# Another order for the first block of layer 1, between a full attention and a full expert network

## The chip, the cores and the metric

The kernel runs on one core of one Trainium2 chip. The metric is the time of the whole program on the device, in microseconds, as the median of three runs. The engines of the core are named as in the profile: PE is TensorE's matrix multiplication (PEld its loading of weights), DVE is VectorE, ACT is ScalarE, POOL is GpSimd, SP is the engine that issues most transfers. Each engine works off its own instructions in the order of the program and waits for the others by semaphores.

## The reference, cut to what matters

The input x has 32 rows of 128 tokens with 256 features, 4096 tokens in all. Layer 0 is attention with 8 heads over all tokens. Its output is projected (`out_w`) and added to x. Layer 1 works on the result t, in two steps, each behind a normalisation over the features:

```python
# layer 0, end
ctx = jnp.einsum('bhqk,bkhd->bqhd', attn, V).reshape(Bz, L, Dz)
dec = (ctx @ out_w.T + out_b).reshape(Bz, Nz, Tz, Dz)
x = h + alpha * dec
# layer 1, attention in a window of 24 tokens
t = x.reshape(1, 4096, 256)
key = jnp.einsum('btd,de->bte', ln(t), K)
logits = relu(jnp.einsum('btd,bsd->bts', key, ln(t)) + bias[0])
logits = (logits - 10000.0 * (1.0 - window)) * temperature[0]
t = t + jnp.einsum('bts,bsd->btd', softmax(logits), ln(t))
# layer 1, eight experts of three layers each, weighted by a softmax per token
z = ln(t)
w = softmax(z @ Wr + br)
h = relu(bn1(einsum('bfd,edh->bfeh', z, W1) + b1))
h = relu(bn2(einsum('bfeh,ehk->bfek', h, W2) + b2))
y = einsum('bfeh,ehd->bfed', h, Wo) + bo
t = t + jnp.einsum('bfed,fe->bfd', y, w)
```

`bn` is a scale and a shift per expert and feature, `g * (h - m) / sqrt(v + 0.001) + b`. All arithmetic is in 32-bit floating point.

## The kernel before, in words

**Stages.** The tokens lie in 32 tiles of 128 and in 8 blocks of four tiles (`TPB` is 4). Layer 0's attention is a list of steps (block of queries, group of four heads, tile of keys): `scores` (L1250) multiplies, `exps` (L1265) takes exponentials on ACT, `add` sums them on DVE, and `product` (L1295) multiplies with the values two steps later. In the last block some keys are masked, and POOL sets their exponentials to zero (L1275) before the product. After the last product, `evacuate` copies the attended heads to `big_t`, `close_sums` (L1322) adds up the exponentials on PE, and for this last unit the division is done in three parts, `invert_last` and `scale_last`, for tiles 0 to 4, 5 to 11 and 12 to 31.

Behind that stands the first block of layer 1, written out by hand (L2104 to L2200). It takes twelve tiles through the projection of layer 0 and tiles 0 to 3 through the whole of layer 1's attention to the first layer of the first expert. From then on a loop over 64 pieces of work (a block and an expert) runs. It issues the expert products, and between them, by a planner that reckons with fixed costs and due times, the jobs that prepare the next blocks. The planner knows nothing of measured times, so its order is the same whenever the loop begins.

**The steps of the hand-written block.** `project_half(n, c, ...)` (L1594) multiplies tile n's feature half c with the projection; two halves add up in PSUM. `second(n)` does the half c = 1, which needs the last unit's division. `complete(n)` (L2114, by `finish`, L1608) adds the result to the tokens on DVE and takes their mean and variance. `deviations(ts, 0)` is epsilon and the square root (DVE, ACT), `deviations(ts, 1)` the reciprocal and `nmr`, the negative mean times it, which `normalise` (L1624) on ACT uses. `normalise` also sends the 16 rows at each edge of a tile to its neighbours' buffers by two transfers (SP for the first five tiles, POOL later). `turn` transposes on PE and copies on ACT, `key` multiplies with K, `scores1` and `logits` (L1661, L1672) give the windowed scores of a tile and their maximum on DVE, `exponentials` (L1693) runs on ACT. `turn_weights(p)` (L1699) transposes the weights of two tiles and copies them to `pt`, two parts on ACT and a small third on DVE. `apply` (L1714) multiplies them with the tokens, and `attended` adds the result to the tokens and takes mean and variance again. `expert_tokens` (L1760, tile `xf`) normalises on DVE, `turn_tokens` (L1773) transposes to `xfT`, `layer_halves` (L1844) multiplies two tiles at a time with the first expert's first weights and ends in two rectifiers (`relu`, L1881), `route` (L1787) computes the softmax's inputs and copies them to `lgT` on DVE. `batch_norms` (L1746) makes scale and shift of the batch norms: one square root on ACT, a reciprocal on DVE and four operations on POOL. Behind these in POOL's order stand `with_bias` for tiles 12 to 15 and the weight sums of the first two experts (L1540), whose results SP stores (`kept`). `warm` issues transposes whose results nobody reads.

**PSUM.** Its eight banks are held by four tiles: `one_a` (bank 0), two tiles of three banks, and `one_b` (bank 7). The tiles of three banks are, in turn, the last scores, the sums, `three_a` and `three_b`; a tile takes the place of one whose readers are done. The framework that writes the semaphores keeps the order of two engines' accesses to a PSUM tile. `open_banks` (L1497) closes these pools and opens two others of four banks each; a first write to a new pool waits for the readers of the old ones.

**ACT's tables.** Exponential and square root need different tables. A load stands in front of the first activation that needs another table than the last; copies, rectifiers and scalings run with either.

Of the kernel before, what the change touches and what calls it, by code (L numbers as in the profile page):

```python
# [823 lines left out]
def fast_kernel(ctx: ExitStack, tc: tile.TileContext, ins: dict, out: bass.AP, narrow):  # L824
# [92 lines left out]
    last_parts = []  # L917
    with ExitStack() as l0:
# [296 lines left out]
        with ExitStack() as at:  # L1215
# [167 lines left out]

            stat_at = {
# [17 lines left out]
            for n in range(len(steps) + LAG + 1 + 16):  # L1402
# [22 lines left out]
                if 0 <= n - LAG < len(steps):  # L1425
                    product(*steps[n - LAG])
# [61 lines left out]


    one_a = ps_a.tile([P, BLK], F32, tag="a", name="one_a")  # L1490
    one_b = ps_av.tile([P, BLK], F32, tag="av", name="one_b")
    three_a, three_b = (
        ps_b.tile([P, HG - 1, BLK], F32, tag="b", name=f"three{k}") for k in range(2)
    )
# [78 lines left out]
    def deviations(ts, part):  # L1573
# [8 lines left out]
        nc.vector.reciprocal(rstd0[:, cols], rstd0[:, cols])  # L1582
        nc.vector.scalar_tensor_tensor(
# [9 lines left out]

    def project_half(n, c, ps, start):  # L1594
        nc.tensor.matmul(
            ps, lhsT=big_t[:, c, SIDE + n * P : SIDE + (n + 1) * P], rhs=woT[:, c, :],
            start=start, stop=(c == 1), skip_group_check=True,
        )
# [100 lines left out]
    def turn_weights(p, ps=None):  # L1699
# [11 lines left out]
        nc.vector.tensor_copy(pt[: 4 * SIDE, 2, :], ps[: 4 * SIDE, 2 * P : 3 * P])  # L1711
# [33 lines left out]

    def batch_norms():  # L1746
        def bnp(s):
            k = bn_names.index(s) * 2 * E
            return bnT[:, :, k : k + 2 * E]

        rstd_of(bscale, bnp("v"), 1e-3)
        nc.gpsimd.tensor_tensor(bscale, bscale, bnp("g"), op=ALU.mult)
        nc.gpsimd.tensor_tensor(bshift, bnp("b"), bnp("m"), op=ALU.subtract)
        nc.gpsimd.tensor_tensor(bshift, bshift, bscale, op=ALU.mult)
        nc.gpsimd.tensor_tensor(bshift, bshift, bnp("be"), op=ALU.add)
# [31 lines left out]
    def route(b):  # L1787

        xfT = blk[b]["xfT"]
        ps = bank(f"psr{b}")[:, :P]  # L1790
# [305 lines left out]
    def half(ps, k):  # L2096
        return ps[:, k * D : (k + 1) * D]

    def first_halves(n, ps, k):

        project_half(n, 0, half(ps, k), not k)


    places = [  # L2104
        (one_a, 0), (one_a, 1), (one_b, 0), (one_b, 1),
        (three_a[:, 0], 0), (three_a[:, 0], 1), (three_a[:, 1], 0), (three_a[:, 1], 1),
    ]
    for n, (ps, k) in enumerate(places):
        first_halves(n, ps, k)

    def second(n):
        project_half(n, 1, half(*places[n]), False)

    def complete(n):  # L2114
        finish(n, half(*places[n]))

    invert_last, scale_last = last_parts
    second(0)
# [9 lines left out]
    second(4)  # L2128
    complete(4)
# [10 lines left out]
    warm(one_b, 20)  # L2140
# [10 lines left out]
    complete(TPB + 1)  # L2151
    complete(TPB + 2)

    three_b = ps_b.tile([P, HG - 1, BLK], F32, tag="b", name="three_b")
    for n, (ps, k) in enumerate(((1, 0), (1, 1), (2, 0), (2, 1)), 2 * TPB):
        places.append((three_b[:, ps], k))

    def both(n):
        first_halves(n, *places[n])
# [3 lines left out]
    rows = [(one_a, 0), (one_a, 1), (three_b[:, 0], 0), (three_b[:, 0], 1)]  # L2163
    seen = [scores1(i, half(*rows[i])[:, :BW]) for i in range(TPB)]
    for n in range(2 * TPB + 1, 3 * TPB):
        both(n)
    for i in range(TPB):
        seen[i]()
        exponentials(i)
        if i == 1:  # L2170
            turn_weights(0, one_b)
    complete(2 * TPB - 1)
    attended = apply(0, [one_a[:, :D], one_b[:, :D]])
    turn_weights(1, three_a[:, 0])
    batch_norms()
    attended(0)
    attended(1)
    deviations(range(0, 2), 0)
    attended = apply(1, [one_a[:, :D], one_b[:, :D]])
    deviations(range(0, 2), 1)  # L2180
    expert_tokens(0, 0)
    turn_tokens(0, 0, three_a[:, 1])
# [258 lines left out]
```

## Time and profile before

| what | us |
|---|---|
| median of three runs | 1539.02 (1538.96 to 1543.28) |
| the profiled execution, device time | 1543.32 |
| its span, first to last instruction | 1541.5 |
| last product of layer 0 starts | 738.31 |
| first projection completed on DVE starts | 747.60 |
| first expert product of the loop (psh) starts | 789.67 |
| from there to the end of the span | 751.8 |

The block between the last product and the first expert product takes 51.4 us of the span. In a line of the profile stand start and duration (in the order of time), engine, line of the code, operation, the tiles written and read, and in brackets the idle time of the engine before it with what ended that. Tiles are named without numbers, `three` is `three_a`. A product of 32-bit operands appears as two records. A stretch's line has the busy time of the engines in the order PE, PEld, DVE, ACT, POOL with counts, then TensorE's granted clock as a share of full speed, then the transfers' share and rate.

### The profile page before, as it was taken

How to read it: one execution, taken by the hardware profiler on the slowest of the kernel's cores; microseconds unless marked ns; L12 is line 12 of the kernel's file. 1: busy time of each engine (PE TensorE's matmuls, PEld its weight loads, DVE VectorE, ACT ScalarE, POOL GpSimd, SP SyncE). 2: the span in 40 equal slices, each digit the busy share in tenths (PEclk: the TensorE clock that was granted, in tenths of full speed). 3: DMA queues.
4: the chain of work that ended last, by engine and by line, in shares of the span. 5: the costliest groups of instructions: out<-in, count | busy, mean ns of one | idle time of the engine just before them, and what ended most of it. 6: DMA issues, size and time to landing. Idle time of an engine off the chain costs nothing.

```text
span 1541.5 us, 23828 instructions
## 1 busy us (share of the span) xinstructions
PE 1484.6 (96%) x8877; PEld 840.7 (55%) x8877; DVE 1204.5 (78%) x2203; ACT 937.4 (61%) x1393; POOL 162.0 (11%) x380
## 2 busy tenths in 40 slices
PE   8899899999999999999889999999999999999998
PEld 5333232222222222222547878887877888888887
DVE  3677888989999898999647778677777777777775
ACT  3676687878888888988444445545454444544443
POOL 1111003000000000031053002001010010000000
PEclk8999999999999999999989999999999999999999
DMA  4211101010000010000322333343333433343441
GB/s 117 56 31 27 39 8 31 8 29 9 1 15 8 1 49 15 8 9 1 115 79 93 116 117 106 115 139 107 116 107 112 141 107 117 106 141 111 137 151 64
DMA packets 95976, 110.16 MB, mean 71 GB/s; under 512 B 17527, under 2 KB 84846, under 8 KB 95854
## 3 DMA queue, kind: packets, MB, share of 16 engines
q1 hardware_dynamic: 93008, 106.61, 22.4%
q8 instruction: 72, 1.18, 0.3%
q10 hardware_dynamic: 1150, 1.09, 0.3%
q0 software_dynamic: 1696, 0.87, 0.2%
q14 instruction: 50, 0.41, 0.1%
HBM read 98.87 MB, written 8.53 MB: 70 GB/s over the span
## 4 chain that ended last, share of the span: by engine, by line
PE 72%; DVE 15%; ACT 8%; issue 4%; DMA 0%; POOL 0%; DVEq 0%; ACTq 0%; SPq 0%; POOLq 0%
PE psh L1898 17%; PE sa L1257 14%; PE av L1301 13%; PE psy L1955 10%; DVE acc L1291 3%; ACT h L1883 3%; ACT pt L1271 2%; PE psq L995 2%; PE psv L1010 2%; PE psk L982 2%; PE psk L1654 2%; DVE h L1940 1%; PE sb L1257 1%; DVE tokens L1963 1%; PE psh L1903 1%
## 5 line engine op out<-in xcount | busy, mean ns | idle before, releaser
L1291 DVE TENSOR_TENSOR acc<-acc,pt 128x1024 f32<-128x1024 f32 (+3 forms) x500 | 529.4, 1126 | 40.0 <-ACT pt L1271 28.7
L1271 ACT ACTIVATE pt<-sb 128x1536 f32<-128x1536 f32 (+3 forms) x288 | 387.3, 1345 | 3.3 <-PE sb L1257 3.2
L1257 PE MATMUL sa<-q,kT 32*128 32x512 f32 (+3 forms) x576 | 302.2, 604 | 9.4 <-ACT pt L1269 7.1
L1257 PE MATMUL sb<-q,kT 32*128 32x512 f32 (+3 forms) x1728 | 306.1, 604 | 2.2 <-ACT pt L1271 1.1
L1883 ACT ACTIVATE h<-h,bshift,bscale 128x256 f32<-128x256 f32 x244 | 159.2, 699 | 231.6 <-DVE h L1940 231.6
L1301 PE MATMUL av<-pt,v 128*32 128x512 f32 (+3 forms) x2304 | 286.2, 569 | 3.1 <-POOL pt L1275 1.6
L1955 PE MATMUL psy<-wo,h 128*128 128x256 f32 x1024 | 242.9, 380 | 0.0
L1269 ACT ACTIVATE pt<-sa 128x512 f32<-128x512 f32 (+3 forms) x288 | 162.5, 564 | 92.7 <-PE sb L1257 63.1
L1955 PEld LDWEIGHTS psy<-wo,h 128*128 128x128 f32 x1024 | 191.9, 190 | 30.7 <-issue 5.8
L1257 PEld LDWEIGHTS sa<-q,kT 32*128 32x128 f32 x576 | 84.2, 182 | 220.1 <-ACT pt L1269 180.0
L1301 PEld LDWEIGHTS av<-pt,v 128*32 128x32 f32 x2304 | 45.4, 108 | 202.2 <-issue 182.8
L1963 DVE SCALAR_TENSOR_TENSOR tokens<-psy,w,tokens 128x256 f32<-128x256 f32 x256 | 111.1, 475 | 34.2 <-PE psy L1955 33.7
L1925 DVE TENSOR_TENSOR u<-psh,u 128x256 f32<-128x256 f32 x122 | 51.1, 419 | 101.3 <-ACT u L1924 101.2
L1275 POOL MEMSET pt<- 32x128 f32 (+2 forms) x192 | 58.6, 305 | 635.2 <-ACT pt L1271 541.2
L1883 ACT ACTIVATE h<-psh,bshift,bscale 128x256 f32<-128x256 f32 (+1 forms) x132 | 75.9, 575 | 55.5 <-PE psh L1898 41.3
L1257 PEld LDWEIGHTS sb<-q,kT 32*128 32x128 f32 x1728 | 88.0, 182 | 10.2 <-ACT pt L1271 6.8
L1924 ACT COPY u<-psh 128x256 f32<-128x256 f32 x122 | 44.1, 362 | 78.6 <-PE psh L1898 78.5
L1898 PE MATMUL psh<-tx,s 128*128 128x256 f32 x366 | 89.3, 380 | 0.0
L1898 PE MATMUL psh<-th,s 128*128 128x256 f32 x366 | 89.0, 379 | 0.0
L1940 DVE TENSOR_TENSOR h<-psh,u 128x512 f32<-128x512 f32 x122 | 83.1, 681 | 1.5 <-PE psh L1898 1.4
L1898 PEld LDWEIGHTS psh<-tx,s 128*128 128x128 f32 x366 | 69.2, 190 | 10.4 <-DVE h L1940 0.8
L1898 PEld LDWEIGHTS psh<-th,s 128*128 128x128 f32 x366 | 69.5, 190 | 9.5
(316 smaller groups left out, 1785.6 us busy)
## 6 DMA issues: line engine op xcount, KB each, us to landing
w<-in_L_ffn_W_dram SPq DMA_DIRECT2D x128, 256.0 KB
s<-kept SPq DMA_DIRECT2D x56, 512.0 KB
wo<-in_L_ffn_Wo_dram SPq DMA_DIRECT2D x64, 256.0 KB
xg<-in_x_dram SPq DMA_DIRECT2D x32, 128.0 KB
tokens<-in_x_dram SPq DMA_DIRECT2D x8, 512.0 KB
kept<-s SPq DMA_DIRECT2D x8, 512.0 KB
out_dram<-tokens SPq DMA_DIRECT2D x32, 128.0 KB
rec<-flat SPq DMA_DIRECT2D x60, 64.0 KB
```

The lines of the kernel that those rows point to most:

```text
L1257: nc.tensor.matmul((sb[:, h - 1, :] if h else sa)[:, lo:], lhsT=kT[rows, g, j * P : (j + 1) * P], rhs=q[rows, g, lo:], start=True, stop=True,)
L1269: nc.scalar.activation(pt[:, 0, lo:], sa[:, lo:], AF.Exp, scale=SCALE)
L1271: nc.scalar.activation(pt[:, 1:, lo:], sb[:, :, lo:], AF.Exp, scale=SCALE)
L1275: nc.gpsimd.memset(pt[k * N : (k + 1) * N, :, lo : lo + k * N], 0.0)
L1291: nc.vector.tensor_tensor(live[b, g][:, hs, lo:], old[:, hs, lo:], pt[:, hs, lo:], op=ALU.add)
L1301: nc.tensor.matmul(av[h * HD : (h + 1) * HD, lo:], lhsT=v[:, j, (g * HG + h) * HD : (g * HG + h + 1) * HD], rhs=pt[:, h, lo:], start=(j == ...
L1883: nc.scalar.activation(dst, src, AF.Relu, bias=bshift[:, m, k : k + 1], scale=bscale[:, m, k : k + 1])
L1898: nc.tensor.matmul(ps, lhsT=w, rhs=x, start=start, stop=True, skip_group_check=True)
L1925: nc.vector.tensor_tensor(u, a[:, 1], u, op=ALU.add)
L1940: nc.vector.tensor_tensor(flat.rearrange("p (k c) -> p k c", k=2), self.q, self.u.unsqueeze(1).to_broadcast([P, 2, HB]), op=ALU.add,)
L1955: nc.tensor.matmul(ps[:, i, :], lhsT=ht[:, c, r * P : (r + 1) * P], rhs=wo[k][:, c, :], start=(c == 0), stop=(c == 1),)
L1963: nc.vector.scalar_tensor_tensor(out=tokens(n), in0=ps[:, i, :], scalar=w[:, r, e : e + 1], in1=tokens(n), op0=ALU.mult, op1=ALU.add,)
```

## The change

Nothing is computed differently, except that `nmr` is no longer made where only `expert_tokens` follows, which does not read it. The order of the instructions changes, and with it which PSUM tiles hold what. The first halves of tiles 0, 1, 4 and 5 are issued ahead of layer 0's last product, and only those of 2, 3, 6 and 7 behind the sums. The scores of tiles 0 to 3 come ahead of the projections of tiles 8 to 11, which are split among later steps. Tile 7 is completed ahead of the scores. Two activations of one column, `ready`, load ACT's tables at fixed places. The batch norms' square root stands behind the first expert tokens, their reciprocal and POOL part behind the second. The second `apply` writes into two banks of `three_a`, whose first bank then takes the transposed tokens; `route` uses the third and stands in front of the completion of tiles 8 to 11.

```diff
@@ in layer 0's list of steps
+            def begin_projections():
+                nonlocal one_a, three_a
+                one_a = ps_a.tile([P, BLK], F32, tag="a", name="one_a")
+                three_a = ps_b.tile([P, HG - 1, BLK], F32, tag="b", name="three_a")
+                for n in range(2):
+                    place(n, one_a, n)
+                    place(TPB + n, three_a[:, 0], n)
...
                 if 0 <= n - LAG < len(steps):
+                    if n - LAG == len(steps) - 1:
+                        begin_projections()
                     product(*steps[n - LAG])
@@ deviations, turn_weights, batch norms
         nc.vector.reciprocal(rstd0[:, cols], rstd0[:, cols])
+        if not means:
+            return
...
-        nc.vector.tensor_copy(pt[: 4 * SIDE, 2, :], ps[: 4 * SIDE, 2 * P : 3 * P])
+        copy = nc.scalar.copy if act else nc.vector.tensor_copy
+        copy(pt[: 4 * SIDE, 2, :], ps[: 4 * SIDE, 2 * P : 3 * P])
...
+    def batch_deviations():
+        nc.vector.tensor_scalar(bscale, bnp("v"), 1e-3, None, op0=ALU.add)
+        nc.scalar.activation(bscale, bscale, AF.Sqrt)
+
     def batch_norms():
-        rstd_of(bscale, bnp("v"), 1e-3)
+        nc.vector.reciprocal(bscale, bscale)
         nc.gpsimd.tensor_tensor(bscale, bscale, bnp("g"), op=ALU.mult)
@@ the hand-written block
+    any1 = l1c.tile([P, 1], F32, name="any1")
+    nc.gpsimd.memset(any1, 1.0)
+    def ready(func):
+        nc.scalar.activation(any1, any1, func)
+    one_b = ps_av.tile([P, BLK], F32, tag="av", name="one_b")
+    for n in (2, 3):
+        place(n, one_b, n - 2)
     second(0)
     second(1)
...
     complete(3)
-    second(4)
-    complete(4)
+    for n in (TPB + 2, TPB + 3):
+        place(n, three_a[:, 1], n - TPB - 2)
+    second(TPB)
+    complete(TPB)
...
-    warm(one_b, 20)
+    warm(one_b, 16)
...
     for m, ps in ((0, three_a[:, 2]), (1, one_b)):
         key(0, m, ps)()
-    complete(TPB + 1)
-    complete(TPB + 2)
+    ready(AF.Exp)
+    for n in range(TPB + 1, 2 * TPB):
+        complete(n)
...
+    seen = [scores1(i, rows[i]) for i in range(TPB)]
     both(2 * TPB)
-    seen = [scores1(i, half(*rows[i])[:, :BW]) for i in range(TPB)]
-    for n in range(2 * TPB + 1, 3 * TPB):
-        both(n)
-    for i in range(TPB):
+    both(2 * TPB + 1)
+    for i in range(TPB - 1):
         seen[i]()
-        exponentials(i)
-        if i == 1:
-            turn_weights(0, one_b)
-    complete(2 * TPB - 1)
+        if i < 2:
+            exponentials(i)
+    turn_weights(0, one_b)
+    seen[TPB - 1]()
+    for i in (2, 3):
+        exponentials(i)
     attended = apply(0, [one_a[:, :D], one_b[:, :D]])
-    turn_weights(1, three_a[:, 0])
-    batch_norms()
+    both(2 * TPB + 2)
+    turn_weights(1, three_a[:, 0], act=True)
+    ready(AF.Sqrt)
+    both(2 * TPB + 3)
     attended(0)
     attended(1)
     deviations(range(0, 2), 0)
-    attended = apply(1, [one_a[:, :D], one_b[:, :D]])
-    deviations(range(0, 2), 1)
+    attended = apply(1, [three_a[:, 1, :D], three_a[:, 2, :D]])
+    deviations(range(0, 2), 1, False)
     expert_tokens(0, 0)
-    turn_tokens(0, 0, three_a[:, 1])
+    turn_tokens(0, 0, three_a[:, 0])
+    batch_deviations()
     attended(0)
     attended(1)
     deviations(range(2, TPB), 0)
-    a = layer_halves(blk[0]["xfT"], [one_b, three_a[:, 0]])
+    a = layer_halves(blk[0]["xfT"], [one_b, one_a])
     next(a)
-    deviations(range(2, TPB), 1)
+    deviations(range(2, TPB), 1, False)
     expert_tokens(0, 1)
-    turn_tokens(0, 1, one_a)
+    batch_norms()
+    turn_tokens(0, 1, three_a[:, 1])
+    a = next(a)
+    route(0, three_a[:, 2, :P])
     for n in range(2 * TPB, 3 * TPB):
         complete(n)
     deviations(groups[1], 0)
-    a = next(a)
     open_banks()
     deviations(groups[1], 1)
-    route(0)
```

## The prediction, made before the result was known

> **What bounds the kernel now.** I read the page's busy shares first, then busy time by stretch, then the chain that ended last, then the order of time from 735 to 800 us.
>
> ```profile
> PE 1484.6 (96%) x8877; PEld 840.7 (55%) x8877; DVE 1204.5 (78%) x2203; ACT 937.4 (61%) x1393; POOL 162.0 (11%) x380
> ...
> 747.60:764.00 16.40, 14.48 (x81) 10.82 (x80) 11.91 (x36) 5.69 (x12) 0.00 (x0) 1.00 0.25 77
> 764.00:773.00 9.00, 5.42 (x27) 3.54 (x25) 4.97 (x24) 5.88 (x13) 0.00 (x0) 1.00 0.60 198
> 773.00:783.20 10.20, 8.42 (x21) 5.00 (x22) 9.12 (x24) 0.99 (x3) 9.48 (x17) 0.50 0.14 54
> 783.20:789.70 6.50, 3.12 (x30) 2.13 (x28) 4.05 (x15) 2.24 (x4) 0.00 (x0) 1.00 0.20 81
> 789.70:793.50 3.80, 3.80 (x10) 1.72 (x7) 0.35 (x2) 0.26 (x1) 0.00 (x0) 0.55 0.00 0
> 793.50:850.00 56.50, 55.91 (x237) 38.48 (x236) 32.24 (x93) 31.05 (x61) 25.80 (x40) 1.00 0.31 106
> ```
>
> Columns: stretch, length, busy us of PE, PEld, DVE, ACT, POOL, then the granted clock. From 789.7 TensorE is full (55.91 of 56.50) to the end: what the block before it saves, the end saves. The block, from the last product (738.3) to the first expert product (psh, 789.67), has no full engine: it is one chain through four engines. Its clock is 0.50 from 773 to 783 and again at the entry.
>
> ```profile
> 771.23 1.28 ACT L908
> ...
> 776.43 1.53 DVE xf L1768 x2
> ...
> 781.47 1.69 DVE xf L1768 x2
> ...
> 787.59 1.46 ACT h L1883 x2
> 789.09 0.65 PE psr L1793 x16
> ```
>
> The chain (start, us): the square-root table is on it, xf (the normalised tokens) on VectorE, and the rectifiers (L1883), which stand behind the square root of group 1 on ScalarE.
>
> **The change, part by part**, on the time axis of the profile, span 1541.5.
>
> *Projections ahead.* Eight first halves, 16 records, lie between the sums and the first second half: 743.05 to 746.70. Four go before the last product, where PE waits for POOL: av ends 736.72, the next starts 738.31, a hole of 1.59.
>
> ```profile
> 738.31 1.07 PE L1301 MATMUL av<-pt,v 128*32 128x512 f32 x8 [1.59 <-POOL pt L1275]
> ...
> 744.81 1.89 PE L1595 MATMUL three<-woT,big_t 128*128 128x256 f32 x8
> 747.60 0.42 DVE L1609 TENSOR_TENSOR tokens<-one_a,tokens 128x256 f32<-128x256 f32 x1 [3.50 <-PE one_a L1595]
> ```
>
> Eight records of 0.216 are 1.73, so 0.14 sticks out of the hole; the sums, held by DVE's acc to 742.00, absorb part at most: I charge 0.13. Two stay behind the sums (0.86) while DVE inverts and scales (scale ends 744.10); two go behind complete(3), in PE slack. The second halves of tiles 0 and 1 start at 744.15+0.13, need 0.86 and a fill of 0.17, so complete(0) starts at 745.35 instead of 747.60: **2.25 saved**. From there to the keys the order is the same and DVE and ACT set it. warm() drops from 20 to 16 transposes, 0.44 of PE, before a wait for xl (0.32): nothing on the path while the clock holds. The second key copy ends at 759.35 (now 761.60).
>
> *Scores.* The exp table loads at 759.35 to 760.7, under DVE's complete(5) to (7), which run from 757.65 (they wait for the first key copy) to 760.75. Scores start 759.4, now ahead of tile 8's projection. logits(0) starts 760.7, 0.97 each. The program keeps order between engines over a whole PSUM tile, even where banks differ; the row: complete(5) reads bank 0 of three_a but starts at 759.92, just when ACT's copy of bank 2 (759.30 to 759.89) ends.
>
> ```profile
> 759.30 0.59 ACT L1659 COPY kt<-three 128x512 f32<-128x512 f32 x1 [1.34 <-PE three L1654]
> 759.92 0.43 DVE L1609 TENSOR_TENSOR tokens<-three,tokens 128x256 f32<-128x256 f32 x1 [2.73 <-ACT kt L1659]
> 764.10 1.28 ACT L1696 ACT_TABLE_LOAD   x1 [2.50 <-DVE nm L1690]
> ```
>
> So logits(2) waits until both(8) and both(9) have written three_b: PE 759.4 + 14 score records (1.91) + 8 (1.73) + fill = 763.2; then the small copy of pt (after ACT's), logits(3) 764.75 to 765.8, exp(3) to 766.45. apply(0) is done at 766.3 (the copy's end, 764.8, +1.49 as now). attended(0) starts 766.7 instead of 773.05: **6.35 saved by here**, 2.25 of it the projections, 1.28 the exp table, about 2 the bscale table and root with the recip behind them (771.23 to 773.05), the rest complete(7) and the fewer waits.
>
> *Attended tokens.* Two at 0.97 and their stats end at 768.8. batch_norms leave this place, and with them the POOL queue behind them: with_bias (2.77), eight weight sums (5.8), the memset of w. Beside them two kinds of DVE row are slow now: xf 0.88 against a median of 0.41 in all 32; rstd 0.54 against 0.16. I take 0.41 and 0.16 (all four slow xf lie beside POOL, none of the fast). The second piece of pt goes from DVE to ACT (0.28, like DVE's row), and the sqrt table loads behind the two copies (768.35): 1.28 and a 0.2 dummy, to 769.85, so it holds the root up by 0.9: part of it is *not* hidden. Root, recip, xf x2 end 771.1; transposes, copy of xfT 771.6 to 772.2. attended(2) reads another bank of that same three_a, so by the row above it waits for that copy: 1.1 of idle DVE that the old one_a, one_b did not have. Then two attended (2.2), root (0.6), xf x2 to 775.75, batch_norms' recip and POOL to 777.3 (the rectifier wants it at 777.8), transposes, copy 776.85, second layer half 1.73 to 778.6, route 0.65 to 779.25. The second half and rectifiers no longer stand behind group 1's root.
>
> *What takes a gain back.* route's copy of lgT (DVE) now stands ahead of complete(8) to (11). DVE is free at 776.1, waits for route to 779.3, copies 0.29, and only then does the four completes: three at 0.99 and the last add, 0.39. psh waits for every reader of the old banks, since open_banks closes those pools whole, so it starts at 783.0. In the old block complete(8) ran from 783.08 under PE's layer half, and lgT came last.
>
> ```profile
> 783.08 0.41 DVE L1609 TENSOR_TENSOR tokens<-three_b,tokens 128x256 f32<-128x256 f32 x1
> ...
> 789.67 3.47 PE L1903 MATMUL psh<-xfT,w 128*128 128x512 f32 x4
> 789.87 0.29 DVE L1798 COPY lgT<-psr 128x128 f32<-128x128 f32 x1 [2.04 <-PE psr L1793]
> ```
>
> **The sum:** psh at 783.0 instead of 789.67, so **6.7 us**. SP issues the same transfers in the same order; the weights of work 1 are issued by 762.8 now and asked for 20 us later. Its two kept stores (issued 780.0 to 783.2) wait for POOL's sums and slip with them by 3, and the weights of work 3 behind them; these are wanted some 20 us later. POOL's burst ends near 786.2 instead of 783.0; the memset of w is wanted by psrt's add about 3.5 after psh starts, 786.4: covered by 0.2, and if the clock is full, 1.4 late for ACT's next table, with TensorE fed by other work. The dropped nmr rows (0.17 each, seven blocks) lie beside a full TensorE: nothing.
>
> **Two rules against it.** *The table.* The row: the load at 771.23 stands 0.02 behind a copy (770.84 + 0.37) and its root starts at 772.52, 0.01 behind the load: 1.28 in all. [...] *The clock.* The row: 0.50 from 772.98 to 783.2, after 3.4 us with 19% of PE busy (771 and 772 wholly idle), and 0.50 from 790.0 to 793.46, after 787 to 789 idle; psh took 3.47 where four such take 1.88: 1.6 lost. [...] The new block ends with PE idle from 779.25 to 783.0, 3.7: so a fall at the entry is as likely as now and I leave the 1.6 in. [...]the stretch 773.9 to 777.3 (busy about 1.2 of 3.4) may fall too.
>
> **Time.** The profiled execution took 1543.32 (1.8 around its span); the three runs span 1538.96 to 1543.28, so it is like the slowest of them and 4.3 above the median. Less 6.7 it is 1536.6; the median becomes 1539.02 - 6.7 = **1532.3**. A median of three with such a spread tells no change from one under 0.3% (4.6 us).
>
> **Cases.**
> - *As summed* (0.52): 1532.3, own range 1530 to 1535 for waits read 1 or 2 wrong.
> - *Larger* (0.17): the clock holds at the entry (+1.6) and attended(2) needn't wait (+1.1): 9.4, 1529.6. [...] Against: 3.7 idle.
> [...]
> - *The clock falls inside the block* (0.16): transposes twice 0.45, layer half 1.73, route 0.65 at double time, 3.3 less: 3.4 saved, 1535.6. For: 35% busy in 3.4 us. Against: 0.55 to 0.75 kept 1.00 at 749 to 770.
> - *Nothing* (0.04): the loads' dummies or the banks hold the block at its old length: 1539.
> - *Slower* (0.06), one mechanism: with 4 of 20 warming transposes gone where PE has 0.45 and 0.10 busy (750 to 752), the clock falls there. PE's work from 752.7 to 763 (9.3, less 0.6 of wait) doubles: 8.7 lost; transposes, apply and both up to 772 cost 3.5 more: 12.2 - 6.7 = 5.5 slower, 1544.5. It decides if the half clock lasts beyond about 761. Against: 94% busy brought it back at 783.
>
> Faster by over 0.3%: 0.52+0.17+0.05 = **0.74** (what the first loses over the line the fourth gives back); same 0.16+0.04 = **0.20**; slower **0.06**. The range 1528.5 to 1538.0 leaves out the last two cases and the tails.
>
> **What would show it.** Eight L1595 records before the last av, and complete(0) near 745.3. An exp table load near 759 to 761 and a sqrt load near 768. POOL idle from 740 to 776, xf near 0.4. attended(2) starting with the end of an xfT copy. lgT ahead of complete(8), with idle DVE before it, psh near 783. Wrong if the clock row has 0.5 between 753 and 777, if lgT comes behind the completes, or if psh starts outside 781 to 785.

## The result, and the profile after

Twelve runs of each kernel on one chip: the median went from 1540.85 to **1535.39 us** (1532.92 to 1538.71), a ratio of 0.9966 with a 95% interval of 0.9955 to 0.9976. That is 5.2 us by the ratio, 5.5 between the medians, so faster, by a little more than the 0.3% that was called measurable; the interval reaches to both sides of that line. A second comparison, described below, gave 0.9970 (0.9960 to 0.9980). The forecast was 6.7 us, 1532.3. Of the 3.1 by which the median lies above that, 1.8 is the kernel before: over twelve runs its median is 1540.85, where the three runs known to the forecast gave 1539.02.

The profiled execution took 1538.2 us, with a span of 1536.0 after 1541.5. First the engines' busy line of the page of the changed kernel, then its busy time by stretch, with the columns as before (length; PE, PEld, DVE, ACT, POOL; granted clock; transfers).

```profile
PE 1482.4 (97%) x8873; PEld 839.5 (55%) x8873; DVE 1200.3 (78%) x2193; ACT 938.3 (61%) x1396; POOL 161.9 (11%) x381
```

```profile
745.30:766.40 21.10, 18.52 (x98) 13.27 (x97) 15.95 (x55) 10.00 (x23) 0.00 (x0) 1.00 0.46 148
766.40:776.60 10.20, 7.02 (x36) 4.62 (x34) 6.67 (x23) 3.61 (x9) 0.71 (x3) 0.99 0.07 23
776.60:780.70 4.10, 4.10 (x24) 2.88 (x24) 0.00 (x0) 1.31 (x2) 4.00 (x7) 0.61 0.00 2
780.70:784.60 3.90, 0.01 (x1) 0.00 (x0) 3.52 (x12) 0.25 (x1) 3.82 (x7) 0.82 0.33 134
784.60:790.00 5.40, 5.32 (x7) 2.29 (x8) 1.76 (x8) 1.53 (x3) 0.85 (x3) 0.50 0.24 97
790.00:850.00 60.00, 59.41 (x252) 41.31 (x251) 33.43 (x94) 32.38 (x64) 25.78 (x40) 1.00 0.30 101
```

From the first completed tile (745.4) to 776.35 the clock holds at full speed, where the kernel before had 0.50 from 773 on, and POOL is idle nearly throughout. Then come the three stretches that take gain back. The second layer half runs at half the clock: the clock is 0.50 from 776.35 to 779.76, which with the route behind it, at full speed again, makes the 0.61 of the stretch. After them TensorE is idle for 3.9 us while DVE completes tiles 8 to 11. And the loop's first 5.4 us run at 0.50. The order of time shows the same steps one by one (start, duration, and in brackets the idle time before it and what ended that):

```profile
737.32 0.99 POOL L1276 MEMSET pt<- 32x128 f32 x3 [14.57 <-ACT pt L1272]
738.10 0.59 PE L1393 MATMUL three_a<-woT,big_t 128*128 128x256 f32 x2
738.63 1.06 PE L1302 MATMUL av<-pt,v 128*32 128x512 f32 x8
745.37 0.42 DVE L1627 TENSOR_TENSOR tokens<-one_a,tokens 128x256 f32<-128x256 f32 x1 [1.22 <-PE one_a L1393]
...
768.08 1.28 ACT L2130 ACT_TABLE_LOAD   x1
769.91 0.73 DVE L1791 TENSOR_SCALAR xf<-tokens,mean,rstd 128x256 f32<-128x256 f32 x2
771.79 0.48 DVE L1748 SCALAR_TENSOR_TENSOR tokens<-three_a,sum,tokens 128x256 f32<-128x256 f32 x1 [1.06 <-ACT xfT L1805]
776.58 2.07 PE L1873 MATMUL one_b<-xfT,w 128*128 128x256 f32 x4 [0.68 <-ACT xfT L1805]
780.06 0.65 PE L1816 MATMUL three_a<-xfT,Wr 128*32 128x128 f32 x16
780.84 0.29 DVE L1821 COPY lgT<-three_a 128x128 f32<-128x128 f32 x1 [5.17 <-PE three_a L1816]
781.05 0.42 DVE L1627 TENSOR_TENSOR tokens<-three_b,tokens 128x256 f32<-128x256 f32 x1
784.68 3.75 PE L1926 MATMUL psh<-xfT,w 128*128 128x512 f32 x4 [3.98 <-DVE tokens L1627]
```

Two xf take 0.73 instead of 1.53 or 1.69; attended(2) starts with the end of xfT's copy; lgT stands ahead of complete(8) behind 5.17 of idle DVE; psh waits 3.98 for the last complete. Counted from the start of the last product, which is 738.31 before and 738.63 after, the two profiled executions divide like this (psbo is the bias product of the loop, and its first addition to the tokens is a fixed point where TensorE has been full for a while; psy is the product of an expert's last layer):

| stretch | before | after | saved |
|---|---|---|---|
| start of the span to the last product | 738.31 | 738.63 | -0.32 |
| last product to psh | 51.36 | 46.06 | 5.30 |
| psh to the first psbo addition | 20.03 | 20.95 | -0.92 |
| from there to the last psy addition | 725.84 | 724.55 | 1.29 |
| from there to the end | 5.98 | 5.79 | 0.19 |
| span | 1541.52 | 1535.98 | 5.54 |

The first entry is for the most part the change itself. The last product waits for three memsets of POOL. In the kernel before they stand at

```profile
737.27 0.99 POOL L1275 MEMSET pt<- 32x128 f32 x3 [14.58 <-ACT pt L1271]
```

and the product starts 0.05 behind their end; in the changed kernel it starts 0.32 behind it, as the projections put ahead of it end only at 738.69. So 0.27 of the 5.30 in the second entry is only a later origin, and the block is shorter by 5.0. The last addition of the sums on DVE does not move with the product (from the product's start to the end of that addition it is 3.63 before and 3.36 after).

Two more entries ask for a cause: the 0.92 lost at the entry, and the 1.29 saved in a loop whose order is the same.

### The profile page after: what moved, and what is told of

It is laid out like the page before. It is cut to its first block, busy times and chain, and to the rows that moved or that the text cites. A ratio compares the mean times of both kernels' runs of the same rounds, so it can differ in the third digit from the quotient of the medians.

```text
span 1536.0 us, 23813 instructions
## 1 busy us (share of the span) xinstructions
PE 1482.4 (97%) x8873; PEld 839.5 (55%) x8873; DVE 1200.3 (78%) x2193; ACT 938.3 (61%) x1396; POOL 161.9 (11%) x381
## 4 chain that ended last, share of the span: by engine, by line
PE 74%; DVE 13%; ACT 8%; issue 4%; DMA 1%; POOL 0%; ACTq 0%; DVEq 0%; SPq 0%; POOLq 0%
PE psh L1921 18%; PE sa L1258 15%; PE av L1302 13%; PE psy L1978 11%; DVE acc L1292 3%; ACT h L1906 2%; PE psq L996 2%; ACT pt L1272 2%; PE psv L1011 2%; PE psk L983 2%; PE psk L1672 2%; PE sb L1258 1%; PE sums L1329 1%; PE psh L1926 1%; DVE h L1963 1%
```

## The experiments

In all of them, "from the last product" means from the start of its matmul records (av), so that what differs ahead of the block drops out; against the kernel before, 0.27 of each difference is the later product. The ratios are to the kernel before, run on the same chip beside each.

### The changed kernel once more

No edit; its profile beside the first tells what varies between executions of one program.

> The changed kernel once more, as it is, on the chip of the run beside it. [...]every start of DVE and ACT from the last product to the second copy of xfT is where it was within 0.1 (complete(0) 6.74, attended(0) 27.83, second copy's end 37.90 behind the last product's start); only what TensorE does at half clock (the second layer half, route, the entry) moves, by 0 to 1.5 ahead of psh and by 0 to 3 behind it. The ratio to the kernel before 0.9955 to 0.9976. If other things vary (transfers, DVE), the block's own starts differ too.

Measured: 1536.92 us, ratio 0.9970 (0.9960 to 0.9980). Complete(0), attended(0) and the second copy of xfT stand at 6.75, 27.83 and 37.90, the first profile's values within 0.01. Here psh comes at 46.07 and psbo 20.96 behind it, with the same course of the clock as in the first profile: 0.58 from 776.6 to 780.7 (0.61 there) and 0.50 from 784 to 790. So DVE and ACT repeat to a hundredth. That TensorE's clock is what varies has to come from other runs, and the first of them is the next one.

### nmr made again in the loop

```diff
-        job(("devt", b), 0, lambda b=b: deviations(tiles(b), 1, False), ("devt0", b))
+        job(("devt", b), 0, lambda b=b: deviations(tiles(b), 1), ("devt0", b))
```

> The changed kernel, but the loop makes nmr again for expert_tokens, which does not read it (seven rows of DVE, 0.17 each). The prediction: nothing, for they lie beside a full TensorE; every tile of psh to the end as in the changed kernel. The rival, from the two traces: in the kernel before TensorE waited in front of the transposes of xf at 861.4 (0.43 between the ends of the product before and the transposes), in the changed kernel it does not, and the lead of the changed kernel grows from 4.07 at 850 to 5.36 at 1440 in steps of 0.2 to 0.6, one a block: then this kernel is some 1.3 us slower than the changed one, all of it lost in these steps and none before 850.

Measured: 1536.09 us, ratio 0.9973 (0.9965 to 0.9982), which alone can't tell 1.3 us. The trace can: from the first psbo addition to the last psy addition it takes 725.96, against 725.84 in the kernel before and 724.55 and 724.59 in the changed one. (In the run with the projections alone, which makes nmr too, it is 725.92, and in no trace without nmr over 724.69.) **1.4 us, by the dropped nmr alone**, lost in steps at each block's xf. At the first of them, in the order of time of the kernel before, then of the changed kernel, then of this one:

```profile
861.39 0.59 PE L1898 MATMUL psh<-tx,w 128*128 128x256 f32 x2
862.09 0.76 PE L1778 MATMUL ptf<-ident,xf 128*128 128x128 f32 x4
```

```profile
857.32 0.59 PE L1921 MATMUL psh<-tx,w 128*128 128x256 f32 x2
857.75 0.60 PE L1801 MATMUL ptf<-ident,xf 128*128 128x128 f32 x4
```

```profile
853.72 0.59 PE L1921 MATMUL psh<-tx,w 128*128 128x256 f32 x2
854.48 0.76 PE L1801 MATMUL ptf<-ident,xf 128*128 128x128 f32 x4 [0.16 <-DVE xf L1791]
```

From the start of one product to the start of the transposes it is 0.70, 0.43 and 0.76. TensorE is "full", but the planner issues the transposes right behind xf, and xf stood behind nmr on DVE; a late xf is TensorE's idle time at once. The transposes themselves then take 0.76 instead of 0.60, as they follow the second xf.

This run, whose block is instruction for instruction that of the changed kernel, also shows the block with its clock held at the place that matters: the second copy of xfT ends at 37.94, lgT starts at 40.70 and psh at **44.54**, 1.52 ahead of the first profile. Its clock fell as well, but for 3.4 us from 769.67, under the first layer half, whose result is not yet waited for (a stretch of this run, columns as above):

```profile
769.70:773.10 3.40, 3.40 (x10) 2.36 (x10) 2.92 (x11) 0.20 (x1) 0.00 (x0) 0.50 0.02 5
```

Between this execution and the first, the last product's start differs by 2.4 us too (736.22 and 738.63). That lies in the first 30 us of the program, long before the change; the granted clock in the changed kernel, then in this one:

```profile
20.00:25.00 5.00, 5.00 (x12) 2.98 (x13) 0.00 (x0) 0.59 (x1) 0.00 (x0) 0.50 0.05 0
```

```profile
20.00:25.00 5.00, 4.42 (x24) 2.53 (x22) 2.31 (x6) 0.65 (x2) 0.00 (x0) 0.79 0.04 2
```

Half the clock here and 0.79 there for the same instructions: layer 0's steps start 2.84 apart at 30 us, and 2.4 at 734. The lead shrinks at one place, by 0.45 between 160 and 180 us, where this run's clock was 0.50 from 168.9 to 172.3.

### Transposes that keep the clock

```diff
     next(a)
+    warm(three_b[:, 0], 10)
     deviations(range(2, TPB), 1, False)
...
     turn_tokens(0, 1, three_a[:, 1])
+    warm(three_b[:, 0], 5)
     a = next(a)
     route(0, three_a[:, 2, :P])
+    warm(one_b, 30)
```

> The changed kernel with transposes that nobody reads, in TensorE's idle time: 10 behind the first layer half, 5 behind the second transposes of tokens, 30 behind route (0.107 each at full clock: 1.1, 0.5, 3.2). They compute nothing. The theory that the clock explains what is between runs of one program and what the changed kernel's profile lost against the sum: the granted clock stays 1.00 from the last product to the loop; from the last product's start to psh 44.5 (46.06 in the changed kernel, 44.54 in the run with nmr, which held its clock there), from psh to the first psbo's add 18.3 (20.95 in the changed kernel): 4.1 less together, and the median 2 to 4 below that of the changed kernel, as some of its runs lose less. The rival: the idle time is no cause of the fall (it comes by itself), the clock falls all the same, and the transposes delay what stands behind them: same or slower by up to 3.

Measured: 1534.05 us (1532.22 to 1534.53), ratio 0.9957 (0.9942 to 0.9971). From the last product to psh 44.50, from psh to psbo 18.31, both as expected. The two stretches in which the changed kernel's clock was down, in this kernel:

```profile
776.60:780.70 4.10, 3.97 (x38) 3.05 (x37) 0.76 (x3) 2.11 (x3) 3.94 (x9) 1.00 0.00 2
784.60:790.00 5.40, 5.40 (x17) 2.73 (x16) 2.41 (x13) 4.10 (x8) 2.33 (x6) 1.00 0.36 146
```

The clock is 1.00 where the changed kernel had 0.61 and 0.50. It is one execution, but up to the block its clock takes the course of the first profile: its last change, early in layer 0, lies 713.1 ahead of the last product, there 713.2. In each of the seven traces here whose TensorE stands idle for the completes ahead of psh (3.98 in the changed kernel's) the clock fell at the entry. So in these traces the fall goes with TensorE's idle time and did not come where work without use filled it, and against this run the falls cost the changed kernel's profile 1.56 in the block and 2.64 at the entry. The median gained less than these 4.2, about 1.4 to 2 us by the ratios, known to about 2; the expectation of 2 to 4 holds at its lower end at best. Not every execution loses the 1.56, as the nmr run shows, and keeping the clock here does nothing for the first 30 us.

### Projections ahead alone

The kernel before with one part of the change:

```diff
+                    if n - LAG == len(steps) - 1:
+                        begin_projections()
                     product(*steps[n - LAG])
...
+    one_b = ps_av.tile([P, BLK], F32, tag="av", name="one_b")
+    for n in (2, 3):
+        place(n, one_b, n - 2)
     second(0)
```

> The kernel before with one part of the change: the first halves of tiles 0, 1, 4, 5 ahead of the last product, those of 6 and 7 behind complete(3). The theory of the prediction: complete(0) starts at 745.35 instead of 747.60 on that kernel's axis, and as DVE and ACT set the order from there to the keys and the chain has no slack behind them, psh starts 2.2 earlier too, near 787.4; the time is 2.2 us (0.14%) below the kernel before, give or take the clock. The rival: a later wait (the exponential's table, POOL's burst or a clock that falls at another place) holds the block, so complete(0) is 2.2 early and psh less than 1 early; then most of the change's gain comes from its other parts.

Measured: 1539.16 us, ratio 0.9986 (0.9979 to 0.9992): **2.2 us**. Complete(0) comes at 6.75 instead of 9.29 and psh at 49.14 instead of 51.36. Without the 0.27 of the later product that is 2.3 and 1.95 earlier. The rival, that a later wait holds the block, is out, although TensorE ran at half clock for longer here (770.1 to 787.2) than in the kernel before. From psh to psbo it took 18.34, so this execution kept its clock at the entry, without any warming.

### Batch norms where they were

```diff
     ready(AF.Sqrt)
+    batch_deviations()
+    batch_norms()
...
     turn_tokens(0, 0, three_a[:, 0])
-    batch_deviations()
...
     expert_tokens(0, 1)
-    batch_norms()
```

> The changed kernel with the whole of the batch norms where the kernel before has them: epsilon, root, reciprocal and POOL's operations ahead of the first attended token, the square root's table still loaded ahead of them. By the rows of the changed kernel: the load's dummy ends 30.95 behind the last product's start, bscale's root 31.2, its reciprocal 31.6, so the first attended token starts at 31.6 instead of 27.83, its pair's xf at 34.5 instead of 31.28: 3.2 later, as the root of the tokens no longer waits for the table. POOL's burst then lies beside DVE from 31.6 to 42.5: with the slowed rows of the run with the norms one step earlier (0.35 for rstd, 0.2 a piece of xf) each pair loses 0.6 to 0.9, so the second copy of xfT ends 4.0 to 5.0 later, at 42 to 43, and with the same clock the time is 4 to 5 above the changed kernel, near the kernel before. The rival: the norms' place is worth the 1.3 of the one-step run alone, since the table on the chain is the same: under 2 later.

Measured: 1541.47 us, ratio 1.0002 (0.9992 to 1.0012): **no faster than the kernel before**. The first attended token starts at 31.38, the xf at 34.52 (3.24 later), the second copy of xfT ends at 42.81 (4.91 later). The rows divide the 4.91:

```profile
773.70 1.15 DVE L1791 TENSOR_SCALAR xf<-tokens,mean,rstd 128x256 f32<-128x256 f32 x2
...
778.50 0.62 DVE L1599 TENSOR_SCALAR rstd<-mean 128x2 f32<-128x2 f32 x1
...
779.59 1.29 DVE L1791 TENSOR_SCALAR xf<-tokens,mean,rstd 128x256 f32<-128x256 f32 x2
```

The xf start 3.24 later; the two pairs of xf take 0.41 and 0.55 longer and one rstd 0.45, all beside POOL; and the first transposes, at half clock here, cost 0.26. By the median, nothing is left of the change's gain without this one move. The profile leaves a little: psh at 49.41 is 1.95 ahead of the kernel before, 1.7 without the 0.27 of the later product; the entry (21.10) takes 1.07 of it, and the loop gains its 1.3 by the dropped nmr. The median, sure to about 1.5 us, shows nothing of these 1.9; with the projections' 2.2 and the completes behind route in the same block, what is left is within what the clock's course moves.

### Batch norms one step earlier

```diff
     batch_deviations()
+    batch_norms()
     for k in range(2):
         attended(k)
...
     expert_tokens(0, 1)
-    batch_norms()
```

> The changed kernel, with the batch norms' reciprocal and their POOL part one step earlier: behind the first transposed tokens, where DVE waits for the copy of xfT, instead of behind the second xf. So POOL's burst (four operations, with_bias, weight sums, near 11 us) starts near 772.3 and lies beside the second pair of xf at 774.7. If two engines that work at once slow each other (as the xf rows of the kernel before suggest: 0.88 beside POOL, 0.41 without): the reciprocal's 0.45 and twice 0.45 for xf and some 0.3 for reciprocal and root's TENSOR_SCALAR, xfT's second copy 1.3 to 1.7 later, time up to 1.7 slower. If the slow rows of before had another cause: 0.45 slower at most, xf 0.37 each.

Measured: 1538.38 us, ratio 0.9982 (0.9973 to 0.9991). Behind the first copy of xfT attended(2) starts 0.43 later here instead of 0.03, as the reciprocal stands ahead of it; the second copy ends 1.31 later. By the ratios the time is 1.8 to 2.5 longer than the changed kernel's, where up to 1.7 was expected; they are known to about 2. Most of the 1.31 that is not the reciprocal is in two rows, the view of the tile xf and the order of time in this kernel:

```profile
L1791 DVE TENSOR_SCALAR xf<-tokens,mean,rstd x2: 414/616/819, 774.0 to 774.4; 128x256 f32<-128x256 f32 x2
...
772.14 2.89 POOL L904 TENSOR_TENSOR tokens<-tokens,outb 128x256 f32<-128x256 f32 x4
773.04 0.52 DVE L1599 TENSOR_SCALAR rstd<-mean 128x2 f32<-128x2 f32 x1
```

One xf of 819 ns beside POOL, and rstd of 0.52 instead of 0.17. In the changed kernel the 32 xf have a median of 406 ns and a maximum of 412:

```profile
L1791 DVE TENSOR_SCALAR xf<-tokens,mean,rstd x32: 398/406/412, 769.9 to 1406.2; 128x256 f32<-128x256 f32 x32
```

POOL's work beside it does slow these two kinds of row, but not each of them. The other xf of the pair took 0.41 beside POOL too, and there one of POOL's four additions took 0.85 instead of 0.72 (2.89 together, 2.77 in the kernel before). Nor does any work of POOL's do it: the prediction has none of the fast xf of the kernel before beside POOL, but the four near 924 lie beside POOL's operations on a single number, and took 0.40 to 0.41. And not all of DVE's rows are slowed: BN_STATS of a tile takes 0.43 beside POOL and without it. What decides which of the rows is slowed, no run here shows.

### Without the two loads ahead

```diff
-    ready(AF.Exp)
...
-    ready(AF.Sqrt)
```

> The changed kernel without the two activations of one column that load ACT's tables ahead. The theory of the prediction, by the row of 1.28 for a load: the exponential's load then stands behind the first maximum of the logits and its exponential, so exp(0) to the first attended token come 1.0 to 1.3 later (27.8 from the last product's start to 28.8 to 29.1), and the square root's load stands behind rstd's TENSOR_SCALAR, so the root comes 1.3 behind it instead of 0.63: xf 1.6 to 2.0 later in all. [...] The rival that the loads are hidden anyway: under 0.5.

Measured: 1536.93 us, ratio 0.9976 (0.9967 to 0.9985). **The exponential's load made no difference**: attended(0) at 27.82, as in the changed kernel. The square root's made 0.74 (xf at 32.02 instead of 31.28). The first is explained by where the load stands. The lines are of the view of one line of code, in the kernel before and in this one:

```profile
L1696 ACTq EVENT_SEMAPHORE  x1: 17/17/17, 764.1 to 764.1; - x1
L1696 ACT ACT_TABLE_LOAD  x1: 1283/1283/1283, 764.1 to 764.1; - x1
```

```profile
L1714 ACT ACTIVATE s<-s,nm,temp x4: 519/520/521, 762.3 to 766.3; 128x160 f32<-128x160 f32 x4
...
L1714 ACT ACT_TABLE_LOAD  x1: 1283/1283/1283, 759.9 to 759.9; - x1
```

In the kernel before a wait of its own stood ahead of the load, so the load began only when the logits' maximum was there. Here the load began at 759.9, behind the copy of kt, 2.35 before its exponential, with no activation put there to call it. The other changes in the order had already taken the separate wait away. At the square root such a wait does stand ahead of the load in this kernel, and that is the 0.74:

```profile
L1602 ACTq EVENT_SEMAPHORE  x1: 17/17/17, 769.4 to 769.4; - x1
L1602 ACT ACT_TABLE_LOAD  x1: 1283/1283/1283, 769.5 to 769.5; - x1
```

The exponential in the kernel before and the root here start within 0.02 of the load's end, so of a switch these rows show the load's 1.28 and nothing beside it.

### First transposed tokens in another tile

```diff
-    turn_tokens(0, 0, three_a[:, 0])
+    turn_tokens(0, 0, one_a)
```

> The changed kernel, with the first transposed tokens in one_a instead of the first bank of three_a. The prediction's step: attended(2) reads another bank of that three_a and so waits for the copy of xfT (1.06 of idle DVE in the changed kernel's trace). Here it should start as soon as DVE is through with bscale's TENSOR_SCALAR, 1.0 earlier against the start of the first xf (0.85 instead of 1.88 behind it), and the second copy of xfT and the first expert product 1.0 earlier, if the clock takes the same course. The rival: the wait was for something else (PE's transposes, the apply), and the distance stays 1.88.

Measured: 1531.89 us, ratio 0.9950 (0.9932 to 0.9968). In the order of time:

```profile
770.87 0.17 DVE L1770 TENSOR_SCALAR bscale<-bnT 128x32 f32<-128x32 f32 x1
770.96 0.47 DVE L1748 SCALAR_TENSOR_TENSOR tokens<-three_a,sum,tokens 128x256 f32<-128x256 f32 x1
771.49 0.59 ACT L1805 COPY xfT<-one_a 128x512 f32<-128x512 f32 x1 [1.50 <-PE one_a L1801]
```

Attended(2) starts ahead of the copy instead of behind it, 0.74 behind the first xf instead of 1.88, and the second copy of xfT ends 1.15 earlier. So the wait was for another engine's access to another bank of the same tile. It cost a little more than the 1.06 of its row. The ratio is 2.5 us below the changed kernel's (known to about 3), more than this wait explains; the clock, which did not fall in the block in this trace and cost 1.70 at the entry, can be the rest.

### Completes ahead of route

```diff
     turn_tokens(0, 1, three_a[:, 1])
-    a = next(a)
-    route(0, three_a[:, 2, :P])
     for n in range(2 * TPB, 3 * TPB):
         complete(n)
+    a = next(a)
+    route(0, three_a[:, 2, :P])
```

> The changed kernel, with the four completes of tiles 8 to 11 ahead of the second layer half and route instead of behind route. The prediction named this order as what takes a gain back: DVE is idle from 775.7 to 780.8 in the changed kernel, and the four completes (3 x 0.99 + 0.39 to the last add) came only then. Here they should start near 775.7, end near 779.7, and psh start with the lgT copy, near 781.4 instead of 784.65: 3.2 earlier. As TensorE then is idle for 0.7 instead of 3.9 ahead of psh, the clock should hold at the entry, which is worth up to 2.65 more (in the changed kernel TensorE was busy for 5.3 at half its clock there): the time 3 to 6 us below the changed kernel. The rival: psh waits for something else as well (the second rectifier, the lgT copy behind a slow route, weights), and gains under 1.

Measured: 1532.34 us, ratio 0.9941 (0.9926 to 0.9956). Psh at 42.69, 3.37 ahead of the changed kernel's profile, although the second layer half ran at half clock here as well. The entry took 19.39, 1.56 less than there, and its rest is no clock:

```profile
781.54 0.29 DVE L1821 COPY lgT<-three_a 128x128 f32<-128x128 f32 x1 [1.33 <-PE three_a L1816]
...
786.10 0.19 DVE L1832 TENSOR_TENSOR w<-psrt,br 128x32 f32<-128x32 f32 x1 [3.01 <-POOL w L1829]
```

DVE had been idle 5.17 in front of lgT and is so for 1.33 now. In its place DVE waits 3.01 for the memset of w, which stands last in POOL's burst.

### Three moves together, and a fourth

```diff
+    ready(AF.Sqrt)
     turn_weights(1, three_a[:, 0], act=True)
-    ready(AF.Sqrt)
...
-    turn_tokens(0, 0, three_a[:, 0])
+    turn_tokens(0, 0, one_a)
...
+    for n in range(2 * TPB, 3 * TPB):
+        complete(n)
     a = next(a)
     route(0, three_a[:, 2, :P])
-    for n in range(2 * TPB, 3 * TPB):
-        complete(n)
```

> The changed kernel with three moves together: the four completes ahead of the second layer half, the first transposed tokens in one_a, and the square root's table ahead of the copies of pt (ACT is idle there for 1.2 of the load's 1.28). From the last product's start to psh: the changed kernel's sum with a held clock is 44.5; less 3.3 for the completes (route's end + 0.29 + 0.25 decides, not the adds), less 1.0 for one_a, less 0.6 to 0.9 for the table: 39.5 to 40. If the clock falls nowhere the entry takes 18.3 to the first psbo's add. Against the kernel with the completes alone (1532.3): 1.5 to 3.5 faster, near 1529.5. The rival: DVE becomes the chain (attended, xf and the completes in one queue without idle time), and only one of the two smaller moves counts: under 1 faster.

Measured: 1532.06 us, ratio 0.9945 (0.9928 to 0.9961). Psh at 39.61, as expected. But from there to psbo it took 22.43, and the sum (62.04) is that of the completes alone (62.08): all of the 3.1 saved ahead of psh was given back behind it, and of the 1.5 to 3.5 us expected over the completes alone nothing shows in the medians. The row that says where:

```profile
782.87 0.19 DVE L1832 TENSOR_TENSOR w<-psrt,br 128x32 f32<-128x32 f32 x1 [4.37 <-POOL w L1829]
```

The fourth move is to let POOL clear w ahead of its burst:

```diff
+    def open_shares(b):
+        blk[b]["wide"] = fx.tile([P, TPB, HD], F32, tag="w", name=f"w{b}")
+        nc.gpsimd.memset(blk[b]["wide"], 0.0)
...
     expert_tokens(0, 0)
+    open_shares(0)
```

> The three moves of best1, and POOL's memset of w for the first block ahead of POOL's burst instead of behind its weight sums. In best1 the first expert product came 39.6 behind the last product, but from there to the first psbo's add it took 22.4 instead of 18.3: w's first add waited 4.37 for that memset, behind it on DVE stood pso's add, on ACT the exponential's table, and TensorE ran dry for 2 us and lost its clock. If this is the cause, the way from psh to psbo is 18.3 to 18.6 here, the sum 58 from the last product's start (62.0 in best1, 67.0 in the changed kernel's profile, 62.8 with its clock held), and the time 3 to 4.5 below best1, near 1528. If TensorE runs dry for another cause (the square root of group 1, which DVE and ACT reach at 777 to 778, then tiles 4 to 8's transposes): 62 again, and no faster than best1.

Measured: **1528.24 us** (1525.93 to 1529.71), ratio 0.9914 (0.9899 to 0.9928). Psh at 39.63, psbo 18.32 behind it, the sum 57.95; the changed kernel beside it took 1536.92. The same addition here:

```profile
779.55 0.19 DVE L1837 TENSOR_TENSOR w<-psrt,br 128x32 f32<-128x32 f32 x1 [0.92 <-PE psrt L1830]
```

It waits for TensorE's psrt now and not for POOL. The clock is 1.00 from 765 to 800, with no warming added. This version beats both kernels.

## Why the prediction was right, and where its terms were off

The steps of the chain, from the last product, in us (the prediction's times less 738.31; "held" is the nmr and keep runs, whose clock held there):

| step | predicted | changed kernel | held |
|---|---|---|---|
| complete(0) | 7.04 | 6.74 | 6.75 |
| logits(0) | 22.4 | 22.06 | 22.06 |
| attended(0) | 28.4 | 27.83 | 27.83 |
| first copy of xfT ends | 33.9 | 33.13 | 33.13 |
| second copy of xfT ends | 38.5 | 37.90 | 37.90 to 37.94 |
| lgT starts | 41.0 | 42.22 | 40.66 to 40.70 |
| psh starts | 44.7 | 46.06 | 44.50 to 44.54 |

The prediction left the last product where it was. It came 0.27 later, so 0.27 has to be added to the measured columns to compare them with the first.

**The sum ahead of psh** was right: 6.7 predicted, 6.6 with a held clock (6.8 from the last product's start, less the 0.27). About 0.25 of it is the clock of the kernel before: from the end of its first pair of xf to the copy of xfT it took 0.77 at half clock, where the changed kernel took 0.52. Its larger mechanisms have runs of their own. Of the 6.6 that the first attended token is earlier, the projections ahead make 2.3 and the batch norms' place, with the square root and the table in front of it, 3.5; the other 0.8 (the exponential's table, complete(7), the place of the scores) no run divides. At the second copy of xfT the batch norms' place is worth 4.9, of which slower xf and rstd beside POOL are 1.41 (0.41, 0.55 and 0.45). Attended(2) waits for a copy of its tile, 1.15 with what follows. The order of lgT and the completes took back what it was charged. Of the small lead at each step (0.2 to 0.8 in the table) 0.27 is the later origin; what is left is 0.03 at complete(0), 0.5 at the first copy of xfT and nothing at psh. The hole did not hold all eight records, and the product was late by more than the 0.13 charged; but the sums, which wait for DVE, took that up whole, as the prediction said they might in part.

**The clock in the block** was named as a case of its own, at 3.3 us, with a chance of 0.16. It came in the first profile, from 776.35 and not from 773.9, so that only the second layer half ran at it: 1.5 us in place of 3.3. Of the six other executions here in which the layer halves follow the first copy of xfT in the changed kernel's order (again, nmr, loads, onea, norms, completes), three fell at this place, so 0.16 was too small.

**The clock at the entry** was left at the 1.6 of the kernel before. It measured 2.64 in the changed kernel's profile, against 1.72 in the kernel before by the same count (20.03 less 18.31). The reason is in the rows: psh at half clock lasted from 784.7 to 790.0 here, where it had lasted from 790.0 to 793.5. In the seven executions whose TensorE waits for the completes (the two of the changed kernel, nmr, norms, oldnorms, loads, onea) the loss is 1.65 to 3.04, in no case nothing; the larger case with a held clock (0.17) was put too high.

**"The dropped nmr rows: nothing"** is the step that failed by its reasoning, and it was paid in the other direction: 1.4 us saved in the loop. The cover was named (a full TensorE), but TensorE's own next instruction was waiting for the row behind nmr.

**The exponential's table** was counted at 1.28 for loading it ahead. The load did leave the path, but not by the activation put there for it. The chance of 0.05 in the forecast's sum for "faster" stood for a switch of tables dearer than its row; the runs show 1.28.

So 6.6 in the block and 1.4 in the loop, less 1.5 in some executions and about 1 at the entry, is 5.5 to 7.0, against 5.2 (3.7 to 6.9) by the ratio; in the profiled pair 5.54. That the total came as near to the forecast is in part luck: the 1.4 of the loop, put at nothing, covers a good part of what the clock took. The slower rival, a clock that falls near 750 as there are fewer warming transposes, did not come: the row from 745.3 to 766.4 has 1.00. Of the three signs that were to show the prediction wrong one came, if barely: the clock is 0.50 from 776.35, within 753 to 777. LgT stands ahead of the completes, and psh, at 784.68, lies within 781 to 785.

What stays open is how far the clock's course in the first 30 us, which differs between executions, hides or adds to a difference of 1 us between medians; no run here sets it.

## What to carry to other kernels

Before a row beside a "full" engine is costed at nothing, look at what stands behind it on its own engine, and whether the full engine's next instruction reads that: seven rows of 0.17 were worth 1.4 us. When a move makes a wait shorter, ask what the engine would have done meanwhile and which queue now ends last: here the completes filled DVE's idle time, and then a memset at the end of POOL's queue cost all that two further moves had saved. Where one engine's work starts and stops at the microsecond, count its idle time as a cost of its own, since it can be paid as half the clock on the products that follow: here 1.65 to 3.04 us at the entry, in the seven traces that idle ahead of psh.

## What the runs showed of the hardware that was not expected

The granted clock makes executions of one program differ by microseconds, and nothing else was seen to: in the first 30 us (2.84 apart), in the block (1.5) and at the entry (1.65 to 3.04 against 18.31), while DVE and ACT start at the same hundredth. In the twelve executions of the changed kernel the time goes with the mean granted clock: the three with 0.993 took 1538.3 on average, the three with 0.996 took 1533.3, and 0.003 of a span of 1536 us is 4.6, near the 5.0 between them (an estimate from these figures). In the changed kernel's profile the clock changes in the block and at the entry at 776.35, 779.76, 783.18 and 790.00, which is 3.41, 3.42 and 6.82 from one change to the next; in that of the kernel before at 772.95, 783.19, 790.02 and 793.43, which is 10.24, 6.83 and 3.41. The nmr run's fall lasted 3.4 too, and it began 33.5 behind the last product, where that of the changed kernel's profile began 37.7 behind it: the same instructions met it at different places. The keep run adds that the fall goes with idle time: with the idle 1.3 and 0.7 ahead of the second layer half filled, the clock stayed at 1.00 through it. How much idle time it takes is not shown, and the busy share that the profile gives does not tell: in the 3.41 ahead of the nmr run's fall TensorE was busy for 2.24, while in the run with the first transposed tokens in another tile the clock stayed at 1.00 behind 3.41 (from 776.73) with 1.57 busy. So the prediction's reading that a share of 0.55 to 0.75 keeps the clock is no rule.

In these traces a table's load stands behind a semaphore wait of its own where the trace shows one ahead of it (764.1 before, 769.4 in the run without loads), and ahead of the wait where it shows none (759.9): 1.28 on the path or hidden. What puts the wait there the traces do not say.
